# Pairwise products of each row: the second half of the input loaded later, by GpSimd, between its products

## The chip, the cores and the metric

The kernel runs on one core of a Trainium2 chip. The metric is the device time of one execution in microseconds (us). Before the change it is 1267.64 us, the median of three executions (1267.57 to 1267.8).

The engines that matter here are VectorE (DVE in the profile), GpSimd (POOL), ScalarE (ACT, only at the start) and SyncE (SP, which issues the stores). The data is moved by 16 DMA engines, which the core's queues share: one queue is fed by SyncE's requests (q1, "hardware_dynamic"), one by GpSimd's (q0, "software_dynamic"). A "q" after an engine's name (POOLq) is the engine's own sequencer: waits, branches, semaphores, drains.

## The reference

For every row of a 4096 x 256 array in float32, all products of two of its elements are computed, and the upper triangle is kept, row by row:

```python
B, D = (4096, 256)
d = inputs.shape[1]
dot = jnp.einsum('bi,bj->bij', inputs, inputs)
iu, ju = jnp.triu_indices(d)
return dot[:, iu, ju]
```

A row of 256 values (1 KB) becomes 32,896 values (131.6 KB). In all 4.2 MB are read and 539 MB written.

## The kernel before

**Tiling.** Each of the 128 partitions has 32 rows of the input. A *unit* is two rows in each partition (`each` = 512 floats, 2 KB in a partition, 256 KB over all), so the whole input, tile `x` (`xt` in the code), has 16 units, 32 KB in a partition. Two units form one of 8 *passes* (h = 0 to 7). The output of a unit, 2 x 32,896 floats in a partition, is cut into three *pieces* at even borders, so a pass has six pieces, p = 0 to 5: 10,944 or 11,008 columns for two rows, 11.2 MB over all partitions. Pieces are written alternately into two tiles, the *places* `o0` and `o1` (both shown as `o`), and stored from there by one request of SyncE. A request's 128 partitions are spread over the 16 DMA engines, 8 partitions for each; in a large store an engine moves 16 packets of about 44 KB.

**Who computes.** A product of one element with the rest of its row is one `tensor_tensor` (two rows at a time). VectorE copies the pass's unit into `xv` (SBUF) and `xp` (PSUM) at L208 and computes most of a piece at L229 with one operand from each. GpSimd computes the rest of the piece at L283, both operands from `xv`. The first two pieces of all, p = 0 and 1 of pass 0, are made by VectorE and ScalarE (L255) instead, and piece 0 is stored in five parts so that the stores begin early (cuts at `FIRST`).

**The order.** There is no scheduler: every engine runs its own loop (L328) over h, and the waits are written out by hand. An iteration has pieces 2 to 5 of pass h and then pieces 0 and 1 of pass h + 1. VectorE begins a piece when the store that last used its place has landed on all 16 DMA engines (semaphores `free`, L216 and L218) and lets GpSimd go (`go`). When both are done (`v_done`, `g_done`), SyncE issues the store (L309). So at any time one store is running while the next piece is computed. At the end of every third piece GpSimd releases `x_read` (L296), after which VectorE may overwrite `xv` (L206).

**The input.** SyncE loads unit 0, units 1 and 2, and unit 9 (L350, `NEAR`), over all 16 DMA engines. The other twelve units, 3 to 8 and 10 to 15, are loaded at the start of the program by GpSimd, in ten requests (L356, `FAR`): nine of 14 partitions each (every ninth partition) and one of 2, with 2 x 12 KB for each partition. Ahead of each of the nine, and once at the very beginning with 5 rows, GpSimd issues a small request that reads 2 x 256 B for each of 2 rows into a scratch tile (`mark`, L360; `marks` is read by nobody). [...]

**The end.** SyncE takes the remaining semaphores (L376 to L382; it waits for the input loads of GpSimd there too, though they landed long before), every engine drains, and a barrier ends the program (L159, L406).

Of the kernel before, what the change touches and what calls it, by code (L numbers as in the profile page):

```python
# [12 lines left out]
P = 128  # L13
# [1 line left out]
REPEAT = 2  # L15
PIECES = 3
EDGE = 32
NEAR = [(0, 1), (1, 3), (9, 10)]
FAR = [3, 10, 6]
COMB = 9  # L20
FORE = 5
MARK = 64
PLACES = 2
SETS = 2
# [39 lines left out]
def interleave(block: list) -> list:  # L64


    sets, k = [], 0
    for left in range(SETS, 0, -1):
        share = -(-len(vector_ops(block[k:])) // left)
        end = k  # L70
        while end < len(block) and len(vector_ops(block[k : end + 1])) <= share:
            end += 1
        if left == 1:
            end = len(block)
        sets.append(vector_ops(block[k:end]))
        k = end
    order, last = [], {}
    for step in range(max(map(len, sets))):
        for s, ops in enumerate(sets):
            if step < len(ops):  # L80
                order.append((*ops[step], last.get(s)))
                last[s] = len(order) - 1 if ops[step][1] == 2 else None
    return order


def schedule(order: list) -> dict:


    waits = {}
    for k, (*_, before) in enumerate(order):  # L90
        if before is not None and before > max(waits.values(), default=-1):
            waits[k] = max(before, k - 2)
    return waits
# [21 lines left out]
def window(ap: bass.AP, free: list) -> bass.AP:  # L115
    return bass.AP(ap.tensor, ap.offset, [list(ap.ap[0]), *free])
# [3 lines left out]
def kernel(  # L120
# [15 lines left out]
    nc = tc.nc  # L136
    n, d = x.shape
    width = out.shape[1]
    each, groups = REPEAT * d, n // (P * REPEAT)
# [8 lines left out]
    x_in = x.rearrange("(p g) d -> p (g d)", p=P)  # L148
# [5 lines left out]
    xt = pool.tile([P, passes, rounds * each], F32, name="x")  # L154
    xv = pool.tile([P, each + 1], F32, name="xv")
    marks = pool.tile([P, 2, 2 * MARK], F32, name="marks")
# [4 lines left out]
    def semaphore(name: str):  # L161
        return ctx.enter_context(nc.semaphore(name))

    free = [semaphore(f"free{k}") for k in range(PLACES)]
    head, v_done, a_done, go = (semaphore(s) for s in ("head", "v_done", "a_done", "go"))
    loaded = [semaphore(f"loaded{k}") for k in range(len(NEAR))]
    far, marked = semaphore("far"), semaphore("marked")
    teeth = P // COMB
    rest = P - COMB * teeth
    landings = [*((sem, 16) for sem in loaded), (far, 16 * (COMB + 1)), (marked, 16 * (COMB + 1))]  # L170

    def take(engine, sem, value: int):
        engine.wait_ge(sem, value).then_inc(sem, -value)  # L173
# [7 lines left out]
    def blocks(p: int, ahead: bool):  # L181

        lo, hi = spans[p % PIECES]
        cuts = [lo, *(FIRST if ahead and p == 0 else []), hi]
        for a, b in zip(cuts, cuts[1:]):
            block = runs(d, a, b)
            if ahead:
                k = split(block)
                yield a - lo, b - lo, block[:k], block[k:], lo
            else:  # L190
                k = next(k for k in range(len(block)) if gpsimd_time(block[k:]) <= BUDGET * 1e3)
                yield a - lo, b - lo, block[k:], block[:k], lo
# [56 lines left out]
    def scalar(pieces: range):  # L249

        xa = xt[:, 0, :each]
        for p in pieces:
            for _, _, block, _, lo in blocks(p, True):
# [12 lines left out]
                else:  # L266
                    nc.scalar.sem_inc(a_done, 1)

    def gpsimd(h, pieces: range, ahead: bool):

        done = turns = 0
        for p in () if ahead else pieces:
            place = places[p % PLACES]
            ((_, _, block, _, lo),) = blocks(p, False)
            turns += 1
            nc.gpsimd.wait_ge(go, turns)
            order = interleave(block)
            waits = schedule(order)
            counted = {len(order) - 1, *waits.values()}
            number = {k: done + 1 + c for c, k in enumerate(sorted(counted))}  # L280
            for k, ((i, j, at, length), m, _) in enumerate(order):
                at -= lo
                ins = nc.gpsimd.tensor_tensor(  # L283
                    place[:, :, at : at + m * length],
                    window(xv[:, j:], [[d, REPEAT], [1, m], [1, length]]),
                    window(xv[:, i:], [[d, REPEAT], [1, m], [0, length]]),
                    ALU.mult,
                )
                if k in waits:
                    ins._wait_ge(g_own, number[waits[k]])  # L290
                if k in counted:
                    ins.then_inc(g_own, 1)
            done += len(counted)
            nc.gpsimd.wait_ge(g_own, done).then_inc(g_done, 1)  # L294
            if (p + 1) % PIECES == 0:
                nc.gpsimd.sem_inc(x_read, 1)  # L296
        if turns:
            nc.gpsimd.sem_inc(g_own, -done)
            nc.gpsimd.sem_inc(go, -turns)

    def sync(h, pieces: range, ahead: bool, done: int = 0) -> int:
        for p in pieces:
            place = places[p % PLACES]
            parts = list(blocks(p, ahead))
            for lo, hi, *_, base in parts:
                done += 1
                nc.sync.wait_ge(v_done, done)
                to = x_out[bass.ds(h, 1), p // PIECES, :, :, base + lo : base + hi]
                store = nc.sync.dma_start(to.rearrange("o p r c -> p (o r) c"), place[:, :, lo:hi])  # L309
                store._wait_ge(a_done if ahead else g_done, done)  # L310
                store.then_inc(free[p % PLACES] if len(parts) == 1 else head, 16)
        return done

    def settle(done: int, ahead: bool = False):
        nc.sync.sem_inc(v_done, -done)
        nc.sync.sem_inc(a_done if ahead else g_done, -done)

    def all_pieces(engine, pieces_of):
        done = pieces_of(0, range(AHEAD), True)
        if engine is nc.vector:  # L320
            nc.vector.sem_inc(v_own, -done)
        elif engine is nc.sync:
            settle(done, True)
        if engine is not nc.sync:
            for sem, count in landings[1:4]:
                engine.wait_ge(sem, count)
        kind = engine.engine
        with nc.Fori(  # L328
            0,
            passes,  # L330
            engines=OrderedEngineSet([kind]),
            head_slot={kind: 0} if engine is not nc.sync else {},
        ) as h:
            done = pieces_of(h, range(AHEAD, PASS), False)
            with engine.If(h < passes - 1):
                nxt = nc.s_assert_within(h + 1, 0, passes - 1)
                if engine is nc.vector:
                    nc.vector.sem_inc(v_own, -vector(nxt, range(AHEAD), False, done))
                elif engine is nc.sync:
                    settle(sync(nxt, range(AHEAD), False, done) - done)  # L340
                else:
                    pieces_of(nxt, range(AHEAD), False)
            if engine is nc.sync:
                settle(done)
        if engine is nc.vector:
            nc.vector.sem_inc(v_own, -done)

    flat = xt.rearrange("p h d -> p (h d)")
    for (lo, hi), sem in zip(NEAR, loaded):
        nc.sync.dma_start(flat[:, lo * each : hi * each], x_in[:, lo * each : hi * each]).then_inc(sem, 16)  # L350

    def load_far(rows: slice):
        one, two, units = FAR
        free = [[(two - one) * each, 2], [1, units * each]]
        to, of = (window(ap[rows, one * each :], free) for ap in (flat, x_in))
        nc.gpsimd.dma_start(to, of).then_inc(far, 16)  # L356

    def mark(lo: int, hi: int):
        of = window(x_in[lo:hi], [[2 * MARK, 2], [1, MARK]])
        nc.gpsimd.dma_start(marks[lo:hi, :, :MARK], of).then_inc(marked, 16)  # L360

    mark(0, FORE)
    for k in range(COMB):
        load_far(slice(k, k + COMB * (teeth - 1) + 1, COMB))
        mark(FORE + rest * k, FORE + rest * (k + 1))
    load_far(slice(P - rest, P))
    nc.vector.memset(xv[:, each:], 0.0)  # L367
    for engine in (nc.vector, nc.scalar):
        engine.wait_ge(loaded[0], 16)
# [4 lines left out]
    for engine, pieces_of in ((nc.vector, vector), (nc.gpsimd, gpsimd), (nc.sync, sync)):  # L374
        all_pieces(engine, pieces_of)
    take(nc.sync, x_read, 1)  # L376
    for sem in loaded:
        take(nc.sync, sem, 16)
    for sem, count in landings[len(NEAR) :]:
        nc.sync.wait_ge(sem, count)  # L380
    for k in range(PLACES):
        take(nc.sync, free[k], 16 * uses)  # L382

# [26 lines left out]
```

## Time and profile before

| what | value | where it is from |
|---|---|---|
| median of three executions | 1267.64 us | times |
| the profiled execution | 1267.5 us | times |
| its span, first to last instruction | 1265.7 us | page, head |
| VectorE busy | 794.9 us, 63% | page, part 1 |
| GpSimd busy | 777.5 us, 61% | page, part 1 |
| ScalarE busy | 29.2 us | page, part 1 |
| written, read | 538.97 MB, 4.21 MB | page, part 3 |
| 47 large stores, issue to landing | 31.7 to 33.9 us (medians) | page, part 6 |
| ten loads of GpSimd, one issue | 557 to 573 ns, at 2.4 to 12.5 us | trace, L356 |
| ten mark requests, one issue | 567 to 733 ns, at 1.6 to 11.9 us | trace, L360 |

The span leaves 1.8 us of the execution outside it. A "group" in the profile is a run of like instructions of one line: its start, its length, the engine, the line, what it writes and reads, its shape and the number of instructions; in brackets stands how long the engine was idle before it and what ended that. In the rows of "windows" there follow the stretch, its length, each engine's busy time (with the number of instructions), the granted clock, the busy share of the 16 DMA engines together, and the rate in GB/s. A large store takes longer from issue to landing than the 26 us between two stores, since it is issued while the one before it is still running.

### The profile page before, as it was taken

Reading aid. Unit: us, or ns where it says so; the run is one execution under the profiler, and the core shown is the slowest. Engines: PE = TensorE matmul, PEld = TensorE weight load, DVE = VectorE, ACT = ScalarE, POOL = GpSimd, SP = SyncE. Lnnn points to the kernel's source line nnn. Section 1 sums busy time; section 2 is a strip of 40 time slices with the busy share of each in tenths; the row PEclk is TensorE's granted clock in tenths of the full one; section 3 lists DMA queues with packets and bytes.
Section 4 is the critical chain, followed back from the end, with each engine's and each line's share of the span. In section 5 each row is a group of like instructions: output and inputs, shape, how many; then the busy total and the mean of one; then the engine's idle time right before and its main releaser. Section 6 shows DMA issues by size and latency. Waiting matters only on the chain. (4 is left out here: it accounts for less than half of the span.)

```text
span 1265.7 us, 2953 instructions
## 1 busy us (share of the span) xinstructions
DVE 794.9 (63%) x1197; ACT 29.2 (2%) x79; POOL 777.5 (61%) x1052
## 2 busy tenths in 40 slices
DVE  8846856568466674766648665586645856468560
ACT  8000000000000000000000000000000000000000
POOL 3457674676647765577556765667556675576740
DMA  9999999999999999999999999999999999999997
GB/s 368 434 435 432 437 431 434 434 433 433 434 436 431 436 433 433 432 435 437 431 436 430 436 432 435 433 434 437 429 438 430 434 433 434 434 434 436 427 439 319
DMA packets 15383, 543.24 MB, mean 429 GB/s; under 512 B 1401, under 2 KB 1424, under 8 KB 2320
## 3 DMA queue, kind: packets, MB, share of 16 engines
q1 hardware_dynamic: 14576, 540.02, 98.8%
q0 software_dynamic: 800, 3.16, 0.7%
q14 instruction: 7, 0.06, 0.0%
HBM read 4.21 MB, written 538.97 MB: 429 GB/s over the span
## 5 line engine op out<-in xcount | busy, mean ns | idle before, releaser
L229 DVE TENSOR_TENSOR o<-xv,xp 128x512 f32<-128x512 f32 (+61 forms) x1164 | 776.9, 744 | 424.4 <-DMA out_dram<-o 302.4
L283 POOL TENSOR_TENSOR o<-xv 128x292 f32<-128x292 f32 (+60 forms) x1028 | 765.9, 786 | 446.6 <-DVEq L216 309.5
L255 ACT ACTIVATE o<-x 128x253 f32<-128x253 f32 (+38 forms) x78 | 28.0, 450 | 0.0
L208 DVE COPY xv<-x 128x512 f32 (+1 forms) x16 | 6.8, 427 | 10.1 <-DVEq L173 7.2
L208 DVE COPY xp<-x 128x512 f32 (+1 forms) x16 | 11.1, 695 | 0.5
L360 POOL DMA_DIRECT2D marks<-in_r_inputs_dram x10 | 5.8, 585 | 1.2 <-SPq L159 1.2
L356 POOL DMA_DIRECT2D x<-in_r_inputs_dram x10 | 5.6, 560 | 0.0
L255 ACT ACT_TABLE_LOAD x1 | 1.3, 1283 | 4.1 <-DMA x<-in_r_inputs_dram 4.1
L367 DVE MEMSET xv<- 128x1 f32 x1 | 0.1, 59 | 1.0 <-SPq L159 1.0
L397 POOL MEMSET const-float32-0.0<- 128x1 f32 x1 | 0.1, 98 | 0.2 <-issue 0.2
L397 POOL MEMSET const-bfloat16-1.0<- 128x1 bf16 x1 | 0.1, 101 | 0.0
L397 POOL MEMSET const-uint8-127<- 128x1 uint8 x1 | 0.1, 101 | 0.0
L397 POOL MEMSET const-float32-1.0<- 128x1 f32 x1 | 0.1, 98 | 0.0
## 6 DMA issues: line engine op xcount, KB each, us to landing
out_dram<-o SPq DMA_DIRECT2D x31, 10944.0 KB, 33.9
out_dram<-o SPq DMA_DIRECT2D x16, 11008.0 KB, 31.7
out_dram<-o SPq DMA_DIRECT2D x1, 4544.0 KB, 20.8
x<-in_r_inputs_dram POOLq DMA_DIRECT2D x9, 336.0 KB, 5.8
out_dram<-o SPq DMA_DIRECT2D x1, 2816.0 KB, 16.4
out_dram<-o SPq DMA_DIRECT2D x1, 2048.0 KB, 13.6
out_dram<-o SPq DMA_DIRECT2D x1, 1024.0 KB, 11.0
x<-in_r_inputs_dram SPq DMA_DIRECT2D x2, 256.0 KB, 3.7
```

What stands on the lines that cost most here:

```text
L208: ins = nc.vector.tensor_copy(to, x_of(h, p // PIECES))
L229: ins = nc.vector.tensor_tensor(place[:, :, at : at + m * length], window(xv[:, j:], [[d, REPEAT], [1, m], [1, length]]), window(xp[:, i:] ...
L255: nc.scalar.activation(places[p][:, r, at - lo : at - lo + length], xa[:, r * d + j : r * d + j + length], AF.Copy, scale=xa[:, r * d + i ...
L283: ins = nc.gpsimd.tensor_tensor(place[:, :, at : at + m * length], window(xv[:, j:], [[d, REPEAT], [1, m], [1, length]]), window(xv[:, i:] ...
L356: nc.gpsimd.dma_start(to, of).then_inc(far, 16)
L360: nc.gpsimd.dma_start(marks[lo:hi, :, :MARK], of).then_inc(marked, 16)
L367: nc.vector.memset(xv[:, each:], 0.0)
L397: nc = _bacc.Bacc("TRN2", target_bir_lowering=False, num_devices=1)
```

## The change

Two things change in the input's loads.

- SyncE's third load takes units 3 to 7 (five units) instead of unit 9. With it, SyncE loads units 0 to 7, the first half of the input, over all 16 DMA engines.
- GpSimd's loads of the second half, units 8 to 15, are moved from the start of the program into its loop. In pass h = 2 it loads units 8, 9, 12 and 13, and in pass h = 3 units 10, 11, 14 and 15 (`LATE`), each time in ten requests of 14 partitions (the tenth of 2) with 2 x 4 KB for each partition. Five of the ten are issued after its products of piece 2, five after those of piece 3 (`TURNS`). Each is followed by a mark request of two rows, the tenth by one of 14 rows; the very first is preceded by one of 5 rows. That makes 11 requests after piece 2 and 10 after piece 3 in pass 2, and 10 and 10 in pass 3: 41 requests in all, where there were 20.
- After piece 5 of these two passes GpSimd waits for its loads, and in pass 3 it then drains.
- The waits for GpSimd's loads ahead of the loop and at the end of the program go.

The requests after piece 2, and the waits and the drain after piece 5, stand ahead of the release of `x_read`. Products, pieces, places and stores are as before. The diff, in its core:

```diff
-NEAR = [(0, 1), (1, 3), (9, 10)]
-FAR = [3, 10, 6]
+NEAR = [(0, 1), (1, 3), (3, 8)]
+LATE = {2: (8, 12), 3: (10, 14)}
+TURNS = {2: range(5), 3: range(5, 10), 5: ()}
+UNITS = 2
 COMB = 9
-FORE = 5
+FORE, AFT = 5, 14
...
+    def mark(lo: int, hi: int):
+        of = window(x_in[lo:hi], [[2 * MARK, 2], [1, MARK]])
+        nc.gpsimd.dma_start(marks[lo:hi, :, :MARK], of).then_inc(marked, 16)
+
+    def load_late(units: tuple, k: int):
+        one, two = units
+        rows = slice(k, k + COMB * (teeth - 1) + 1, COMB) if k < COMB else slice(P - rest, P)
+        free = [[(two - one) * each, 2], [1, UNITS * each]]
+        to, of = (window(ap[rows, one * each :], free) for ap in (flat, x_in))
+        nc.gpsimd.dma_start(to, of).then_inc(far, 16)
+        if k < COMB:
+            mark(FORE + rest * k, FORE + rest * (k + 1))
+        else:
+            mark(FORE + rest * k, FORE + rest * k + AFT)
+
+    def late(h, p: int):
+        for turn, (when, units) in enumerate(LATE.items()):
+            with nc.gpsimd.If(h == when):
+                if TURNS[p]:
+                    for k in TURNS[p]:
+                        if turn == k == 0:
+                            mark(0, FORE)
+                        load_late(units, k)
+                else:
+                    nc.gpsimd.wait_ge(far, 16 * (turn + 1) * (COMB + 1))
+                    nc.gpsimd.wait_ge(marked, 16 * ((turn + 1) * (COMB + 1) + 1))
+                    if turn + 1 == len(LATE):
+                        nc.gpsimd.drain()
+
     def gpsimd(h, pieces: range, ahead: bool):
...
             nc.gpsimd.wait_ge(g_own, done).then_inc(g_done, 1)
+            if p in TURNS:
+                late(h, p)
             if (p + 1) % PIECES == 0:
                 nc.gpsimd.sem_inc(x_read, 1)
...
         if engine is not nc.sync:
-            for sem, count in landings[1:4]:
-                engine.wait_ge(sem, count)
+            for sem in loaded[1:]:
+                engine.wait_ge(sem, 16)
...
-    def load_far(rows: slice):
-        one, two, units = FAR
-        free = [[(two - one) * each, 2], [1, units * each]]
-        to, of = (window(ap[rows, one * each :], free) for ap in (flat, x_in))
-        nc.gpsimd.dma_start(to, of).then_inc(far, 16)
...
-    mark(0, FORE)
-    for k in range(COMB):
-        load_far(slice(k, k + COMB * (teeth - 1) + 1, COMB))
-        mark(FORE + rest * k, FORE + rest * (k + 1))
-    load_far(slice(P - rest, P))
...
-    for sem, count in landings[len(NEAR) :]:
-        nc.sync.wait_ge(sem, count)
```

## The prediction

> **What bounds the kernel now.** I read the page first (part 2 for the DMA, part 5 for what the compute engines wait for), then the timeline of VectorE for the period of the loop, then short windows at both ends of the span, then the instructions of the closing barrier.
>
> ```profile
> DMA  9999999999999999999999999999999999999997
> GB/s 368 434 435 432 437 431 434 434 433 433 434 436 431 436 433 433 432 435 437 431 436 430 436 432 435 433 434 437 429 438 430 434 433 434 434 434 436 427 439 319
> ...
> q1 hardware_dynamic: 14576, 540.02, 98.8%
> q0 software_dynamic: 800, 3.16, 0.7%
> ```
>
> The DMA engines are busy from the first slice to the last at some 434 GB/s, 27.1 GB/s for each of 16. VectorE and GpSimd idle over 420 us each and wait for stores to land (part 5). So no compute instruction matters after the start; bytes and anything that stops a DMA engine do. The next view says which DMA engine counts. These are VectorE's groups at the piece p=3 of each of the eight passes; each starts when the store of piece p=1 has landed on all 16 engines.
>
> ```profile
> 68.43 13.72 DVE L229 TENSOR_TENSOR o<-xv,xp 128x1024 f32<-128x1024 f32 x14 [4.11 <-DMA out_dram<-o]
> ...
> 223.69 13.72 DVE L229 TENSOR_TENSOR o<-xv,xp 128x1024 f32<-128x1024 f32 x14 [4.31 <-DMA out_dram<-o]
> ...
> 379.01 13.72 DVE L229 TENSOR_TENSOR o<-xv,xp 128x1024 f32<-128x1024 f32 x14 [4.36 <-DMA out_dram<-o]
> ...
> 534.29 13.72 DVE L229 TENSOR_TENSOR o<-xv,xp 128x1024 f32<-128x1024 f32 x14 [4.34 <-DMA out_dram<-o]
> ...
> 690.12 13.72 DVE L229 TENSOR_TENSOR o<-xv,xp 128x1024 f32<-128x1024 f32 x14 [4.60 <-DMA out_dram<-o]
> ...
> 846.44 13.72 DVE L229 TENSOR_TENSOR o<-xv,xp 128x1024 f32<-128x1024 f32 x14 [4.62 <-DMA out_dram<-o]
> ...
> 1002.75 13.72 DVE L229 TENSOR_TENSOR o<-xv,xp 128x1024 f32<-128x1024 f32 x14 [4.60 <-DMA out_dram<-o]
> ...
> 1159.07 13.72 DVE L229 TENSOR_TENSOR o<-xv,xp 128x1024 f32<-128x1024 f32 x14 [4.61 <-DMA out_dram<-o]
> ```
>
> A pass of six stores takes 155.3 us three times, then 155.8, then 156.3 three times. One DMA engine is about 1.0 us a pass slower than the others, began ahead of them, and from about 600 us on is the last. Two windows show it:
>
> ```profile
> 1258.70:1262.50 3.80, 0.00 (x0) 0.00 (x0) 0.00 (x0) 1.00 0.05 23
> ...
> 36.50:38.10 1.60, 0.63 (x3) 0.00 (x0) 0.00 (x0) 1.00 0.87 375
> ```
>
> At the end only 0.05 of the DMA, some 23 GB/s, is busy for 3.8 us: one engine alone, about 4 us behind. At 36.5 us 0.87 = 14/16 are busy: two engines have nothing to do. They are the two that got no part of GpSimd's input loads; they have finished the first place's stores and wait for the store that SyncE issues at 37.27, just after VectorE's first run of products ends (5.17 + 31.96 = 37.13). Following the completion packets of each store from one store to the next in the trace's DMA records, one of those two becomes the late engine, and from 38.2 us it never pauses. So the end is: VectorE's 37.13, then 47 stores on the slow engine without a gap, then the landing, then the closing barrier:
>
> ```profile
> L159 POOLq DRAIN  x1: 1697/1697/1697, 1263.2 to 1263.2; - x1
> L159 DVEq DRAIN  x1: 17/17/17, 1263.2 to 1263.2; - x1
> ```
>
> GpSimd's drain takes 1.70 us after the last byte, the others' 0.01 to 0.02, and GpSimd's next one (L406) 0.04. This is the only compute-engine time on the path.
>
> **What the Trainium skill says.** "DMA: Bandwidth & Descriptors", section "Why a DMA increments its semaphore by 16 and not by 1": a request from GpSimd uses the largest k up to 16 that divides the slowest dimension, on k consecutive engines from a round-robin cursor, and all 16 engines post a completion whatever the shape. With a cursor at 0, 5 mark rows take 0 to 4, 14 load rows 5 to 2, 2 mark rows 3 and 4, and so on: 3 and 4 get no load. The 14/16 above agrees. The same page, "Queues, rings and completion order", has each engine alternate between its queues by packet; no row here prices the switch by itself. "SBUF — State Buffer", "SBUF: two separate sides": a VectorE operation with two SBUF inputs shuts GpSimd out of the shared port. Here one input (xp) is in PSUM, and the trace agrees: the issues beside products took 557 to 573 ns each (L356). No page prices a drain of GpSimd after DMA requests.
>
> **The change part by part**, against the profiled run's own 1267.5 us (span 1265.7); the median shown is 0.14 above it.
>
> 1. Third SyncE load of 5 units for 1: per engine 8 more 8 KB, 64 KB / 27.1 GB/s = 2.4 us, the slow engine included. Cover: that engine idles from about 36.4 to 38.2, and the small early stores wait for VectorE anyway (SyncE issues them at its pace). The first store of 2 KB rows may start 0.5 us late; nothing is left at 38.2. If the cover failed wholly, +0.6 (2.4 less the 1.8 idle). I take 0.
> 2. GpSimd's early requests go. VectorE's steps to 37.13 depend only on the first load (landed 3.96 us, before the first GpSimd packets at 4.6 in the DMA records) and on its own operations. The other 14 engines lose 225 KB each from the start, and the first place lands some 5 us earlier, so VectorE's 5.68 us wait at 42.81 shrinks. No gain: the slow engine was and is gated at 37.13. I take 0, between -0.3 and +0.2 for the first load's landing.
> 3. GpSimd now issues 11 requests after piece 2 and 10 after piece 3 in pass 2, 10 and 10 in pass 3: 11 x 0.567 = 6.2 us, 10 x 0.565 = 5.7. GpSimd idles 11.3 us before piece 3 and 8.0 before piece 4, so both fit with 5 and 2 us over. Behind the requests of piece 2 stands the release of x (x_read): 14.6 + 6.2 = 20.8 us after the start of the piece, plus branches, where VectorE is done at 20.0. Its two copies slip by about 1 us, inside its own 4.3 us wait. The waits at piece 5 fall a whole pair of stores after the last request (26 us a store; landing took 4.5 to 9.3 us before). The drain there, 1.7 us or, in proportion to 41 requests, 3.5, fits in the 5.4 us that GpSimd is ahead of VectorE in that piece (19.98 - 14.56). All 0.
> 4. The 14 other engines carry 128 rows x 8 KB / 14 = 75 KB a turn, 2.8 us each, 5.5 in all, now within the saturated stretch. In the new kernel all 16 start the first large store together, so by pass 2 the others lead by some two passes x 1.0 to 1.2 = 2.4 us; the first turn takes that lead, the second leaves them about 2 us behind, and the lead is regained by pass 5 or so. The slow engine would wait only if the others fell some 4 us behind (a store is issued about 4 us before it is needed). 0.
> 5. On the slow engine itself: one mark row per request of marks, 11 + 10 = 21 rows of 512 B at 27 ns (the duration of such packets in the trace) = 0.57 us, and its completion for each of 41 requests, with a change of queue. For that I compare 14 to 20 us (413 GB/s, GpSimd's packets mixed in) with 22 to 36 (434). The deficit is 4.8% of 6 us = 0.29 us per engine for about 6 requests, 49 ns each as an upper bound; shorter packets explain nearly half. I take 25 ns: 41 x 25 = 1.03. The lower end is a 9 ns completion packet alone: 0.37. Sum 1.6 us, from 0.9 to 2.6. Before, the same things fell into the slow engine's idle start.
> 6. The drain at the end has no requests left: 1.70 falls to about 0.04, -1.65. If it is not the requests that it pays for, 0.
>
> Sum: 0 + 0 + 0 + 0 + 1.6 - 1.65 = -0.05; 1267.45 in this execution, 1267.6 beside the median. I write 1267.5.
>
> **The rivals.** A. *A request in the saturated stream costs far more* (the slower side). One mechanism: each of 41 requests makes the slow engine break its stream, fetch from another ring and read HBM before it goes on. At 150 ns instead of 25: +5.1, about 1272.6; it decides against the change by more than 0.2% from about 90 ns (41 x 0.09 + 0.57 - 1.65 = 2.6). For it: nothing before shows a 44 KB packet stream broken by such a request. Against: the 49 ns bound.
> B. *The slow engine isn't avoided*: if the cursor is elsewhere, it takes two shares of 75 KB, 5.5 us: 1267.5 + 5.5 + 1.0 - 1.65 = 1272.4. Against it stands the 14/16 with the same row counts and the 14-row mark that returns the cursor to 5.
> C. *The drain stays*: 1267.5 + 1.6 = 1269.1, still no difference.
> D. *The slow engine gains*, because it is slow through sharing with the early load or gets its first large store sooner: it would need 2.5 us, to about 1264.5. Against: its pass takes 156.3 late, when the others wait for it, and its lead shrinks at the same rate early.
>
> **How the numbers follow.** A difference below 0.2% (2.5 us) I count as none. The forecast of parts 1 to 6 has 0.68, C 0.10, A 0.12, B 0.05, D 0.05. Range: the parts' bounds give 1266.3 to 1269.2; C is inside, and A is taken in up to some 100 ns: 1265.7 to 1270.8. Faster is D, 0.05; same is the forecast and C, 0.78; slower is A and B, 0.17.
>
> **What would show it.** The period of p=3 should be near 156.3 us from the first pass on, with about 0.8 us more in each of passes 2 and 3; the closing drain of GpSimd below 0.1 us; the tail with one engine alone shorter, near 3 us; slice 1 below 368 GB/s. A period of 158 or more in passes 2 and 3 speaks for A, or for B if the lone engine at the end is further behind than 4 us. A drain of 1.7 us at the end speaks for C. If the last period is below 156, the slow engine was not what I took it for.

## The result, and the profile after

| | before | after |
|---|---|---|
| median | 1267.58 us (1267.22 to 1268.22, 21 runs) | 1269.21 us (1268.93 to 1269.51, 21 runs) |
| the profiled execution | 1267.5 us | 1268.93 us |
| its span | 1265.7 us | 1267.1 us |

The ratio is 1.0013 [1.0007, 1.0019]: the changed kernel is 1.63 us slower. That lies inside the forecast's range and below the 0.2% that it counted as no change, but the interval of the measurement excludes no change. The forecast's sum was -0.05 us.

The page of the kernel after, parts 2, 3, 5 and 6 (DMA busy share and rate by slice; queues with packets, MB and share; two groups; one row of DMA issues with KB and median us to landing):

```profile
DMA  9999999999999999999999999999999999999998
GB/s 380 394 444 420 442 439 424 441 423 442 422 436 431 430 426 440 428 426 432 437 429 439 429 435 430 436 442 424 438 429 437 439 427 439 426 438 431 435 440 349
...
q1 hardware_dynamic: 14576, 541.07, 99.0%
q0 software_dynamic: 1632, 2.14, 0.5%
...
L281 POOL DMA_DIRECT2D x<-in_r_inputs_dram x20 | 11.5, 576 | 2.4 <-POOL o L315 2.4
L274 POOL DMA_DIRECT2D marks<-in_r_inputs_dram x21 | 12.1, 576 | 0.9 <-POOL o L315 0.9
...
x<-in_r_inputs_dram POOLq DMA_DIRECT2D x18, 112.0 KB, 22.4
```

The DMA is still busy all the way. GpSimd's queue now has 1632 packets for 2.14 MB, and its large loads need 22.4 us from issue to landing in the median. The timeline of VectorE, its groups at the piece p = 3 of each pass:

```profile
66.11 13.72 DVE L230 TENSOR_TENSOR o<-xv,xp 128x1024 f32<-128x1024 f32 x14 [2.72 <-DMA out_dram<-o]
...
221.97 13.73 DVE L230 TENSOR_TENSOR o<-xv,xp 128x1024 f32<-128x1024 f32 x14 [4.25 <-DMA out_dram<-o]
...
377.29 13.72 DVE L230 TENSOR_TENSOR o<-xv,xp 128x1024 f32<-128x1024 f32 x14 [3.77 <-DMA out_dram<-o]
...
535.56 13.73 DVE L230 TENSOR_TENSOR o<-xv,xp 128x1024 f32<-128x1024 f32 x14 [5.26 <-DMA out_dram<-o]
...
694.44 13.73 DVE L230 TENSOR_TENSOR o<-xv,xp 128x1024 f32<-128x1024 f32 x14 [4.33 <-DMA out_dram<-o]
...
849.73 13.73 DVE L230 TENSOR_TENSOR o<-xv,xp 128x1024 f32<-128x1024 f32 x14 [4.32 <-DMA out_dram<-o]
...
1005.67 13.72 DVE L230 TENSOR_TENSOR o<-xv,xp 128x1024 f32<-128x1024 f32 x14 [4.62 <-DMA out_dram<-o]
...
1162.00 13.72 DVE L230 TENSOR_TENSOR o<-xv,xp 128x1024 f32<-128x1024 f32 x14 [4.60 <-DMA out_dram<-o]
```

Take the differences of the starts: 155.9, 155.3, then 158.3 and 158.9 around the two turns of late loads, then 155.3, 155.9 and 156.3. The loop begins 2.3 us earlier than before (66.11 for 68.43) and is 2.9 us later at its last pass (1162.00 for 1159.07). Then the end, by the closing barrier's instructions (duration in ns, start in us):

```profile
L161 POOLq DRAIN  x1: 45/45/45, 1266.1 to 1266.1; - x1
L161 DVEq DRAIN  x1: 17/17/17, 1266.1 to 1266.1; - x1
```

GpSimd's drain has fallen from 1697 to 45 ns. Last, windows of the kernel after at both ends (stretch, length, busy time of VectorE, ScalarE and GpSimd with counts, clock, DMA share, GB/s):

```profile
1261.40:1263.20 1.80, 0.00 (x0) 0.00 (x0) 0.00 (x0) 1.00 0.11 49
1263.50:1265.40 1.90, 0.00 (x0) 0.00 (x0) 0.00 (x0) 1.00 0.05 23
...
36.30:37.80 1.50, 0.52 (x3) 0.00 (x0) 0.00 (x0) 1.00 0.00 0
```

One engine alone (0.05 is 0.8 of 16) still closes the program, two (0.11) until 1263.4. At 36.3 to 37.8 us all 16 stand idle: nothing of the input is left to load, and the first large store has only just been issued.

**The slow engine's account.** The rest comes from the trace's DMA records: every store ends on every engine with a small completion packet, and the late engine's packets can be followed from store to store. The records don't name the engines; an engine is told by where one packet ends and the next begins, and by its pace. Such readings are good to about 0.1 us.

| term | before | after | difference |
|---|---|---|---|
| 12th large store ends on the slow engine | 350.73 us | 350.39 us | -0.34 |
| its remaining 35 stores | 911.85 us | 915.12 us | +3.27 |
| its last data packet | 1262.58 us | 1265.51 us | +2.93 |
| closing drain of GpSimd | 1.697 us | 0.045 us | -1.65 |
| sum of the last two | | | +1.28 |

All of the +3.27 lies between 350.4 and 588.1 us, the time of the late loads; in the passes after it the slow engine takes its former 156.32 us for six stores. It never waited for work there: each store in that time was issued 3.3 to 7.6 us before the first engine ended the one ahead of it. The -0.34 lies within the scatter: SyncE's first large store goes out anywhere between 36.8 and 37.5 us in the runs below, with the loads of before at 36.82 and 37.27. Without it the sum is 3.27 - 1.65 = +1.62, near the 1.63 between the medians. The two profiled executions differ by 1.43 us, where the terms give 1.28; the other 0.15 us, after the last packet, has no account here.

So the drain gave what was forecast and the slow engine lost 3.27 us in place of 1.6. The experiments ask why.

### The profile page after: what moved, and what is told of

It is laid out like the page before. It is cut to its first block, busy times and chain, and to the rows that moved or that the text cites. A ratio compares the mean times of both kernels' runs of the same rounds, so it can differ in the third digit from the quotient of the medians.

```text
span 1267.1 us, 3025 instructions
## 1 busy us (share of the span) xinstructions
DVE 795.2 (63%) x1197; ACT 29.2 (2%) x79; POOL 789.6 (62%) x1073
## 3 DMA queue, kind: packets, MB, share of 16 engines
q0 software_dynamic: 1632, 2.14, 0.5%
## 5 line engine op out<-in xcount | busy, mean ns | idle before, releaser
L281 POOL DMA_DIRECT2D x<-in_r_inputs_dram x20 | 11.5, 576 | 2.4 <-POOL o L315 2.4
L274 POOL DMA_DIRECT2D marks<-in_r_inputs_dram x21 | 12.1, 576 | 0.9 <-POOL o L315 0.9
## 6 DMA issues: line engine op xcount, KB each, us to landing
out_dram<-o SPq DMA_DIRECT2D x16, 11008.0 KB, 31.7
x<-in_r_inputs_dram POOLq DMA_DIRECT2D x18, 112.0 KB, 22.4
```

## The experiments

All were timed in 5 rounds beside the kernel before, whose median was 1267.48 to 1267.68 us in these calls. "Theory" in the expectations is the account above; each names its rival.

**1. The drain alone, in the kernel before.**

```diff
     load_far(slice(P - rest, P))
+    nc.gpsimd.drain()
```

> The kernel before, with one drain of GpSimd right after its twenty requests. If the 1.70 us of the closing drain is what GpSimd pays for requests not yet settled, it falls to about 0.05 us and the kernel is 1.65 us faster than before, near 1265.9 us. Rival: the closing drain costs 1.7 us whatever happened earlier; then the time stays at 1267.6.

1265.79 us (1265.57 to 1266.62), ratio 0.9988 [0.9979, 0.9996]. The closing barrier of this kernel:

```profile
L159 POOLq DRAIN  x1: 52/52/52, 1262.7 to 1262.7; - x1
L159 DVEq DRAIN  x1: 17/17/17, 1262.7 to 1262.7; - x1
```

The drain's 1.65 us come off the total (-1.69). The early drain takes 12.2 us, from 11.4 us on, and costs nothing that can be seen: GpSimd has no product before 42.61 us. This is the fastest of all the kernels here: 1.7 us below before, 3.4 below after.

**2. The changed kernel without its drain.**

```diff
-                    if turn + 1 == len(LATE):
-                        nc.gpsimd.drain()
```

> The changed kernel without its drain. If the drain in pass 3 is what took 1.65 us off the end, the closing drain grows to 1.7 us or more (in proportion to 41 requests, 3.5 us) and the kernel is 1.6 to 3.4 us slower than the changed one, 1270.8 to 1272.6 us. Rival: 1269.2 as before, if waiting for the landings alone settles the requests.

1272.18 us, ratio 1.0038 [1.0024, 1.0051]. Its closing barrier:

```profile
L161 POOLq DRAIN  x1: 3414/3414/3414, 1266.2 to 1266.2; - x1
L161 DVEq DRAIN  x1: 17/17/17, 1266.2 to 1266.2; - x1
```

The drain costs 3.41 us for 41 requests and 1.70 for 20: 83 and 85 ns a request, though the last had landed over 0.6 ms before. The changed kernel pays the same, but in pass 3, where GpSimd waits anyway:

```profile
L299 POOLq DRAIN  x1: 3414/3414/3414, 610.3 to 610.3; - x1
```

That place is worth 3.0 us of medians (1272.18 - 1269.21), 3.3 between the profiled executions.

**3. The same 41 requests at the start of the program**, with the drain behind them and the wait for the loads ahead of the loop, as before.

```diff
+    mark(0, FORE)
+    for units in LATE.values():
+        for k in range(COMB + 1):
+            load_late(units, k)
+    nc.gpsimd.drain()
```

> The changed kernel with the same 41 requests, unchanged in size and order, issued at the start of the program instead of in passes 2 and 3, with the drain behind them. Theory: the slow DMA engine pays some 3 us for them only because they fall in its unbroken stream; at the start they fall in its idle 3 us before the first large store, so about 2.9 us come back: 1266.0 to 1266.6 us. Rival: the cost comes from SyncE's larger third load or from the split as such, not from the place: 1269 us.

1286.77 us (ratio 1.015 [1.0134, 1.0165]), a miss, but not by the cost in question: 41 requests take until 24.9 us to issue, they queue up behind packets of 44 KB, the last of their own packets ends at 59.1 us, and VectorE begins its next products at 63.62 us. The kernel tells nothing of a request's price in the loop.

**4. The second half by SyncE**, in one request behind the fifth early store; GpSimd issues none.

```diff
+            if ahead and p == 0:
+                half = slice(8 * each, 16 * each)
+                nc.sync.dma_start(flat[:, half], x_in[:, half]).then_inc(loaded[-1], 16)
```

> No request of GpSimd at all: SyncE loads the second half of the input in one request over all 16 DMA engines, behind the fifth early store. Theory: each engine has 128 KB more, 4.8 us, of which about 3.5 us fall into the idle time before the first large store; the rest, about 1.3 us, delays the slow engine; the closing drain is short. With 0.3 us from the earlier first load: near 1266.9 us, 2.3 us below the changed kernel. Rival: the load at that place delays the first large store by its full 4.8 us: 1270.4 us.

1272.33 us, ratio 1.004 [1.0026, 1.0054], a miss of the same kind. The timeline of VectorE in this kernel:

```profile
23.52 13.18 DVE L230 TENSOR_TENSOR o<-xv,xp 128x660 f32<-128x660 f32 x19
50.74 19.99 DVE L230 TENSOR_TENSOR o<-xv,xp 128x260 f32<-128x260 f32 x39 [14.04 <-issue]
```

The wait ahead of the loop and what follows it held VectorE for 14.04 us (the same gap after the change is 5.06), and the stores ran dry. Both kernels were made again with the wait moved to where the data is needed: GpSimd waits after piece 5 of pass 2, ahead of releasing `x_read`.

**5. Requests at the start, the wait late** (drain still at the start).

```diff
+            if p == 5:
+                with nc.gpsimd.If(h == 2):
+                    nc.gpsimd.wait_ge(far, 32 * (COMB + 1))
+                    nc.gpsimd.wait_ge(marked, 16 * (2 * COMB + 3))
```

> As the run with all 41 requests at the start, but the wait for them stands where the data is first needed (GpSimd, piece 5 of pass 2) and no longer ahead of the loop. Theory: the slow DMA engine pays for the requests only where they fall in its unbroken stream. At the start it has some 3 us idle, so most of the 3 us come back: 1265.9 to 1267.2 us. Rival: the cost is that of the larger third load or of the split, not of the place: 1269 us.

1279.11 us (1272.05 to 1281.95), ratio 1.0078 [1.0057, 1.0098]: a miss again, and the timeline of GpSimd in this kernel says why:

```profile
24.29 0.57 POOL L274 DMA_DIRECT2D marks<-in_r_inputs_dram  x1
62.65 12.38 POOL L302 TENSOR_TENSOR o<-xv 128x292 f32<-128x292 f32 x30 [37.79 <-issue]
```

GpSimd, done issuing at 24.9 us, begins its products 37.8 us later. What stood between is in the main the drain, whose own row follows: it ends at 56.5 us, after the last packet of the requests (54.4 us). The 6.2 us after it have no account here.

```profile
L378 POOLq DRAIN  x1: 34505/34505/34505, 22.0 to 22.0; - x1
```

**6. Second half by SyncE, the wait late.**

```diff
+            if p == 5:
+                with nc.gpsimd.If(h == 2):
+                    nc.gpsimd.wait_ge(loaded[3], 16)
```

> As the run with the second half loaded by SyncE behind the fifth early store, with the wait moved to GpSimd at piece 5 of pass 2. In that run the load ended at 40.5 to 43.1 us by engine, where the first large store could have begun at 37.8. Theory: the slow engine is late by that, 2.7 us or more, against the kernel before with an early drain (1265.8): 1268.5 to 1271 us. Rival: the idle time hides 3.5 us of the 4.8, then 1266.9 us.

1268.76 us (1268.46 to 1269.21), ratio 1.0007 [0.9999, 1.0016], 2.97 above experiment 1. The load occupies the engines until 40.8 to 42.5 us, where the first large stores began near 38 us in the kernels before and after, and the slow engine ends its data 3.1 us later than in experiment 1 (1265.30 for 1262.15). It has no late request and no drain to pay, so it is the base that the next experiments add to.

**7 and 8. Forty small requests in the loop, on that base**: 10 each after pieces 2 and 3 of passes 2 and 3, of 2 or of 8 mark rows. Of the 80 or 320 rows the slow engine carries 5 or 20, and nobody carries a large piece.

```diff
+                    for k in range(10 * (p - 2), 10 * (p - 1)):
+                        lo = 2 * k % P
+                        at = MARK * (2 * k // P)
+                        of = window(x_in[lo : lo + 2], [[2 * MARK, 2], [1, MARK]])
+                        nc.gpsimd.dma_start(marks[lo : lo + 2, :, at : at + MARK], of).then_inc(marked, 16)
```

> The run before this one (second half by SyncE) with 40 more requests of GpSimd in passes 2 and 3, in the places of the changed kernel's 41, each of 2 mark rows and nothing else: the slow engine carries 5 of the 80 rows and a completion for each of the 40. If each request costs it 66 ns for itself (completion and change of queue), +2.6 to 2.8 us over the run without them. If each mark row that it carries costs 130 to 155 ns and a completion nothing, +0.7. If the cost comes from the input's bytes moving beside the stores, below +0.8.

> As the run with 40 requests of 2 rows, with 8 rows in each: the slow engine carries 20 of the 320 rows, as many as in the changed kernel. If each request costs 66 ns for itself, +3.1 us over the run without them (0.4 more than with 2 rows). If each row costs it 130 to 155 ns and a completion nothing, +2.6 to 3.1, four times the cost with 2 rows. If the cost comes from the input's bytes, below +1.

1270.28 us (ratio 1.002 [1.0013, 1.0028]) and 1270.51 us (1.0022 [1.0014, 1.003]): +1.52 and +1.75 over experiment 6. On the slow engine, in the DMA records from the 12th large store to the 25th, 1.37 and 1.61 us. With 40 requests at c and 5 or 20 rows at r, 40c + 5r = 1.37 and 40c + 20r = 1.61 give r = 16 ns and c = 32 ns. By these the 41 requests and 21 rows of the change cost 41 x 0.032 + 21 x 0.016 = 1.65 us: near the forecast's 1.6, and half of the 3.27. (The medians give 36 and 15 ns, and 1.8 us.)

**9. Requests at the start, wait and drain late** (experiment 5 with the drain moved behind the wait).

> As the runs with all 41 requests at the start, with the drain moved behind the wait at piece 5 of pass 2. In the last of them GpSimd's first products began only at 62.7 us, when its requests, backed up behind the stores' 44 KB packets, had all been served: the drain held it. Theory: with the drain out of the way GpSimd starts at about 42 us, and the slow DMA engine, which has idle time at the start, comes out 2 to 3.3 us below the changed kernel: 1265.9 to 1267.2 us. Rival: the cost does not depend on the place of the requests: 1269 us.

1267.30 us (1266.94 to 1267.69), ratio 0.9997 [0.9989, 1.0006]. GpSimd now starts at 43.68 us. It is 1.9 us below the changed kernel: the same requests cost that much less ahead of the stream than in it. It is still 1.5 above experiment 1: the last packets of the 41 end at 53.9 us, so a part of them still runs into the large stores.

**10. The change's 41 requests in their places, but small.** The loads are cut to 2 x 256 B for each row, into scratch; the second half comes by SyncE as in experiment 6.

```diff
-        free = [[(two - one) * each, 2], [1, UNITS * each]]
-        to, of = (window(ap[rows, one * each :], free) for ap in (flat, x_in))
-        nc.gpsimd.dma_start(to, of).then_inc(far, 16)
+        of = window(x_in[rows, one * each :], [[(two - one) * each, 2], [1, MARK]])
+        nc.gpsimd.dma_start(marks[rows, :, MARK:], of).then_inc(far, 16)
```

> The changed kernel's 41 requests in their places and with their rows, but each load of 2 x 4 KB a row is cut to 2 x 256 B into the scratch tile, and the second half of the input is loaded by SyncE at the start, as in the run without requests (1268.8). The runs with 2 and 8 rows gave 32 ns a request and 16 ns a row on the slow engine. If that is all, +1.65 us: 1270.4 us; then the other half of the 3.3 us that the changed kernel's slow engine lost belongs to the input's bytes moving on the other engines. If the pattern of requests makes the whole cost, +3.3 us: 1272.0 us.

1270.61 us, ratio 1.0025 [1.0015, 1.0036], +1.85 over experiment 6; on the slow engine 1.64 us, against 1.65 worked out. So the requests as such are priced, and a second half of the loss (3.27 - 1.64 = 1.6 us) is missing here, where the loads are small. None of their bytes goes over the slow engine in either kernel.

**11. The late loads over all 16 engines**, as 8 requests of 16 partitions a turn, without marks.

```diff
-TURNS = {2: range(5), 3: range(5, 10), 5: ()}
+TURNS = {2: range(4), 3: range(4, 8), 5: ()}
...
-        rows = slice(k, k + COMB * (teeth - 1) + 1, COMB) if k < COMB else slice(P - rest, P)
+        rows = slice(k, k + 8 * 15 + 1, 8)
```

> The changed kernel with its late loads in requests of 16 partitions, eight a turn, over all 16 engines and without mark requests. The slow engine now carries 64 KB a turn, 2.4 us each, 4.8 in all, and 16 requests at 32 ns, 0.5: 5.3 us in place of 3.3, so 1271.2 us, 2.0 above the changed kernel. Rival: going past the slow engine saves nothing, since the marks cost as much as they avoid: 1269.2 us or less.

1271.25 us, ratio 1.0028 [1.0017, 1.004]; the slow engine lost 5.38 us. It carries 2 x 64 KB there (4.8 us at 27.1 GB/s) and has 16 requests, which at 32 ns are 0.5; nothing is left over, though the pieces on the other engines have their full size. Going past the slow engine is worth 2.0 us (1271.25 - 1269.21), where its bytes alone would be 4.8: the 41 requests and the extra loss eat the rest.

**12. Half the bytes late**: loads of 2 x 2 KB a row; units 9, 11, 13 and 15 come by SyncE at the start.

```diff
-UNITS = 2
+UNITS = 1
...
+    odd = [window(ap[:, 9 * each :], [[2 * each, 4], [1, each]]) for ap in (flat, x_in)]
+    nc.sync.dma_start(*odd).then_inc(loaded[3], 16)
```

> The changed kernel with half the bytes in its 41 late requests: 2 x 2 KB a row instead of 2 x 4 KB (units 8, 12, 10, 14); SyncE loads units 9, 11, 13 and 15 at the start. Of the slow engine's 3.3 us, 1.65 go with the requests and their mark rows. If the other 1.6 go with the bytes that the other engines load, half of it goes: the slow engine loses 2.4 to 2.5 us from the 12th store to the 25th, and the time is near 1268.4 us, as far as the longer load at the start is hidden. If they go with the number of packets on the other engines, which stays the same, 3.3 us and 1269.2.

1267.93 us (1267.73 to 1269.55), ratio 1.0003 [0.9995, 1.0012]; the profiled execution was the longest of them, 1269.55. The slow engine took 913.58 us for the 35 stores, 1.73 more than before: near the price of the requests alone, without half of the extra.

Three readings of the extra 1.6 us were left: the backlog (two batches of loads overlap, and the slow engine meets many waiting completions), the bytes on the other engines, and the size of their pieces. GpSimd's timeline of pass 2 in the changed kernel shows the first:

```profile
351.41 14.56 POOL L315 TENSOR_TENSOR o<-xv 128x292 f32<-128x292 f32 x38 [8.13 <-DVEq L217]
366.86 0.73 POOL L274 DMA_DIRECT2D marks<-in_r_inputs_dram  x1 [0.89 <-POOL o L315]
...
372.89 0.57 POOL L274 DMA_DIRECT2D marks<-in_r_inputs_dram  x1
377.29 17.93 POOL L315 TENSOR_TENSOR o<-xv 128x924 f32<-128x924 f32 x12 [3.84 <-DVEq L217]
...
400.98 0.57 POOL L274 DMA_DIRECT2D marks<-in_r_inputs_dram  x1
404.24 17.59 POOL L315 TENSOR_TENSOR o<-xv 128x704 f32<-128x704 f32 x16 [2.69 <-DVEq L217]
```

The first batch is issued from 366.9 to 373.5 us and the second ends at 401.6, before piece 4 at 404.2: both fit beside the waits. But a load takes 7.8 to 48.3 us to land (median 24.4), so the second batch meets what is left of the first.

**13. Four batches instead of two pairs**: the same 41 requests at full size, five loads after piece 2 in each of passes 1 to 4.

```diff
-                    for k in TURNS[p]:
+                if p == 2:
+                    for k in range(5 * half, 5 * half + 5):
```

> The changed kernel with the same 41 requests, full size, in four batches of ten or eleven after piece 2 of passes 1, 2, 3 and 4 instead of four batches after pieces 2 and 3 of passes 2 and 3. In the changed kernel the second batch of a pass is issued 30 us after the first, while requests of the first still land up to 36 us after their issue; with half the bytes the last landed after 28 us and the slow engine lost only 1.7 us. If the other 1.6 us come from batches that overlap, they go: the slow engine loses 1.7 us in all, near 1267.6 us. If full-size requests that go past the slow engine cost it that wherever they stand, 3.3 us and 1269.2.

1268.57 us (1268.18 to 1268.87), ratio 1.0006 [0.9998, 1.0015]; landing 7.9 to 36.7 us, median 18.5. The slow engine lost 2.54 us, between the two values that the readings gave: 0.7 us of the extra is gone, 0.9 stays.

The loss on the slow engine, in one table:

| requests in the loop | slow engine loses, us | requests and rows at 32 and 16 ns (bytes at 27.1 GB/s) |
|---|---|---|
| the change: 41, pieces of 4 KB elsewhere, in pairs of batches | 3.27 us (3.47 without the drain) | 1.65 |
| the same, four single batches | 2.54 | 1.65 |
| 41, pieces of 2 KB elsewhere | 1.73 | 1.65 |
| 41, pieces of 256 B | 1.64 | 1.65 |
| 16, pieces of 4 KB on all, its own 128 KB | 5.38 | 0.5 + 4.8 |

**What stays open** is where the extra 1.6 us come from. The table suggests the size of the pieces, but two things on record speak against size, or overlap, by itself. Experiment 11 has full-size pieces and no extra. And in the changed kernel nearly all of the extra falls in one turn: from the 12th store to the 18th the requests of pass 2 cost the slow engine 1.04 us (1.01 in experiment 2), near the 0.85 of 21 requests and 11 rows; those of pass 3 cost it 2.23 (2.48), where 20 requests and 10 rows are 0.80. Pieces, batches and overlap are alike in both.

What does differ between the turns is where the slow engine stood. When pass 2's requests came, it was 1.3 to 1.9 us behind 14 of the other 15 (12th store: 348.46 to 349.11 us, and 350.40); when pass 3's came, all 16 were within 0.9 us (18th store: 507.45 to 508.31, the slow one by its pace at 507.76). In experiments 7, 8, 10, 11 and 12, which show no extra, it was then the last by 0.6 to 2.0 us. So size and place changed together in these runs, no run changes the place alone, and the mechanism isn't shown.

## Why the prediction was right or wrong

**The step that failed is part 5**, the slow engine's price for the late requests: 1.6 us (0.9 to 2.6) was forecast, 3.27 measured, and the 1.63 us of the result are that difference. Its working took a request for its completion and a change of queue: 25 ns each, and 27 ns for a mark row. For requests as such this was right in sum (32 and 16 ns; 1.65 us in all, experiments 7, 8 and 10). It had no term for the other 1.6 us, which the slow engine lost almost wholly in pass 3, beside loads that it doesn't carry; the prediction counted those loads in part 4 only, as time of the engines that carry them. That the term is missing is shown, where it comes from stays open. The 49 ns that it called an upper bound held for a request by itself (32 ns), but not for all that a late request brought: (3.27 - 21 x 0.027) / 41 = 66 ns. It was read at the start of the program, from the rate of all 16 engines among small early stores.

**Part 6 held**: -1.65 us by the drain's own row, and -1.69 in the time where it was changed alone, in experiment 1. **Rival C** (the drain stays) is out.

**Part 1 held**: the larger load of SyncE cost nothing that can be seen. The window 36.3 to 37.8 us shows what covers it, and shows more than the prediction had: all 16 engines idle there, not one or two.

**Parts 2 and 3 held**: the slow engine was gated by the first large store, and GpSimd's issues, release and drain fitted into its waits (the timeline above). At the waits of piece 5 there was less room than part 3 had: it took landings of 4.5 to 9.3 us, where the late loads needed up to 48.3 us. GpSimd left the wait of pass 2 at 452.0 us, still ahead of its next products at 457.06. VectorE's wait of 5.68 us ahead of the loop, which part 2 let shrink, was still 5.06 us, at no cost.

**Part 4 held in its zero, not in its picture.** The loaded engines lost about 3 us a turn (the periods 158.3 and 158.9 are 3.0 to 3.6 above 155.3; 2.8 forecast), and no store was late. Fourteen of the others did start level with the slow engine, and 13 of them led it by 1.8 to 1.9 us at the 12th store (2.4 forecast). But one engine was behind all: 1.7 us at the first large store and 2.5 at the sixth. By the records it is the one that carries the program's instruction fetches, seven packets of 8 KB at 0.31 us each, five of them between 13 and 47 us. So it ended the stores last, and after the turns the loaded engines did. The slow engine, which had lost less in the turns than they, is the last only from about 980 us on. Hence "156.3 from the first pass on" was wrong, though the slow engine itself kept that pace outside the turns: the period of p = 3 shows whichever engine is last, and that was another one in each third of the run. The prediction's own test "158 or more speaks for A" misled for the same reason; the 158 is the pace of the 14 engines, which doesn't set the end.

**Rival B** (the slow engine isn't avoided) is out: the first late load stretches one 44 KB packet to 2.2 to 2.7 us on exactly 14 engines, at 372.7 to 373.3 us. Told by their times, the slow engine's own packets of pass 2 are 11 mark rows and no piece of a load; in pass 3 they can't be told apart, but experiment 12, with the same order of requests, paid 0.88 us there, which leaves no room for pieces. Experiment 11 shows what carrying the bytes costs. The count of 14 agrees with the Trainium skill, "DMA: Bandwidth & Descriptors", "Why a DMA increments its semaphore by 16 and not by 1", on which the forecast rested: 14 partitions go to 14 consecutive engines, from a cursor that moves on. That they are consecutive the records don't show. **Rival A** had the direction and the place, but not the size: all that came with a request stayed below its 90 ns (66), and the request by itself cost 32. **Rival D** (the slow engine gains) is out: its pace is 156.32 us for six stores in both kernels.

**The other signs.** The lone tail was forecast near 3 us; it was 2.1 (the next engine ends its data at 1263.44, the slow one at 1265.51), since the turns had brought the others closer. Slice 1 was to fall below 368 GB/s and rose to 380: it is 31.7 us long, and what left with GpSimd's loads was less than what SyncE's larger load and the earlier stores brought.

## What to carry to other kernels

Where the DMA is busy throughout, find the one DMA engine that ends last and count what that engine does, in time of its own: a request that carries it no byte still cost it 32 ns here, and the 41 requests together twice that, for a reason that the runs leave open. Put such requests where the engine idles anyway (the start, in the kernel before) rather than into its stream, even when the issuing engine has room beside its products. Drain the requests' queue where the draining engine has time; a drain before they are served lasts until they are. The drain alone in the kernel before was worth 1.7 us, more than the whole change lost.

## What the runs showed of the hardware

- GpSimd's closing drain grows with the number of its requests, 83 to 85 ns each, long after they have landed; drained once before, it takes 0.045 to 0.052 us. The earlier drain pays the same price (3.41 us for 41 in pass 3), and behind requests that are still queued it also waits for them: 34.5 us in experiment 5.
- In the saturated stream GpSimd's loads land after 24.4 us in the median and 48.3 at most. By the Trainium skill, "DMA: Bandwidth & Descriptors", "Queues, rings and completion order", an engine alternates between its queues by packet. The records agree within a store: on a loaded engine one small packet stands behind each 44 KB packet of 1.62 us, and a load with its mark request is five of them (two of 4 KB, three of 4 or 8 bytes). By an estimate from these figures five loads take 25 x 1.62 = 41 us. Between two stores the small packets run together: 95 of the 140 pieces of the first batch in 1.6 us at 375 us.
- One of the 16 DMA engines is 0.7% slower than the others in the same stores (156.32 against 155.3 us for six). In the trace of every run here one engine ends alone, 1.7 us or more behind the next.
- Instructions behind a wait can be late, it seems for their own fetch: VectorE's group after the first wait of the loop stood idle for 5.06 us after the change, and 14.04 in experiment 4. In both it begins 1.7 us after a packet of the instruction queue ends (40.15 and 41.88 us; 49.04 and 50.74). No run changes the fetch alone.
